# A graph layer on one core: row norm by statistics instructions, and one ScalarE activation per block of nodes

## The chip, the core and the metric

The kernel runs on one core of a Trainium2 chip. The metric is the time of one execution on the device in microseconds. The core has five engines that run their own queues in order and meet through semaphores: PE (TensorE, matmuls), DVE (VectorE), ACT (ScalarE), POOL (GpSimd) and SP (SyncE, here only an issuer of DMAs). ACT and POOL issue DMAs too.

## What is computed

One layer of a graph network with 6,250 nodes, 64 features and 206,250 edges, sorted by their target:

```python
h = jnp.maximum(_layernorm(x, axis=-1), 0.0)          # (6250, 64), no scale, no shift
msg = h[src] + edge_attr_64                            # (206250, 64)
agg = jax.ops.segment_sum(msg, dst, num_segments=6250)
y = jax.nn.relu(agg @ W1 + b1) @ W2 + b2               # 64 -> 128 -> 64
return x + y
```

`_layernorm` is `(x - mean) / sqrt(var + 1e-5)` along the 64 features.

## The kernel before

**The main stage.** The sum over edges of `h[src]` is made without a gather for most edges. Tiles of three target nodes have up to 128 edges each; for each tile a table of counts (how often each source occurs for each target) is built by a matmul of one-hot codes. Six tiles are one step, and there are 311 steps (0 to 310). In step `n`, `count(n)` does six matmuls into PSUM (L839), and ACT copies the counts into `ring` (L845). DVE makes the one-hot rows `hot` ahead of that (`encode` and `rows_of_tiles`, L806 to L825). Fourteen steps make a block of 252 target nodes; from step 16 on, `products` multiplies the counts of the block before by the normed features `h2` (L857). The edges' own features are summed by one-hot matmuls (`chunk_sum`, L423), with the features loaded by `load`. The 24 last groups of edges are handled differently: POOL gathers rows of `h` from a table in memory and adds them to the edges' features (`fetch_h`, 188 indirect DMAs of L283), and PE sums them (`features_h`, L479). When a pair of such groups comes into PE's order is set by a planner: `clock(n)` gives the assumed start of step `n`, `pool[0]` the assumed time on POOL, which starts at `clock(2) + OPENING_US`, each gather counts 2.0 us, and a pair is taken at one of the steps 5 and 11 of a block for which its last gather is 4 us past. The program's order is written out by hand on every engine, and each engine keeps to it.

**The opening.** Before step 0 the kernel

- loads targets (`dstn`, `firsts_i`), sources (`src`) and `x` (`xl`, by SP in one piece of 6,144 rows and a rest);
- finds for every third target node in which row of 256 targets it begins (`firsts` to `row_i`, matmuls `pf` of L270 and L271), fetches these rows in 15 indirect DMAs (`fetch_row`), and searches them on ACT (`seek`, a Sign activation with a sum, L298); `place` (DVE, L303 and L305) turns the result into edge numbers, three rows at a time;
- transposes the sources on PE (`psrc`, L561), copies them on ACT (L562), packs them with the targets into one word each on DVE (L572), and writes the words to memory (`packed`); `fetch_pair` gathers words by the found edge numbers, `unpack_pair` (DVE, L648 to L667) splits them, and `turn` transposes the digits on PE (`pk`, `pw`) and copies them on ACT into `kq` (L688) and `kv` (L692, an Exp);
- finds where the chunks of edges begin (`chunk_starts`, `chunk_rows`, `chunk_columns`, `chunk_index`);
- norms `x`. The nodes are laid out as 128 partitions by HI = 49 blocks of 64 features, taken in three parts of 16, 16 and 17 blocks.

The norm before takes these steps, all on wide tiles: `norm_mean` (DVE, one reduction over the 49 blocks, L502), `norm_center` for each part (DVE, subtracts the mean, L507; ACT squares, L509), `norm_var` (DVE, a reduction for each part, L514), `norm_root` (DVE, then Sqrt on ACT, L518), `norm_scale` (DVE, reciprocal and one Newton step, L522 to L526), and `norm_h` for each part (DVE, L530: maximum with 0, times the reciprocal root; then SP writes the part to `table`, L531, from which POOL gathers).

The program order ahead of step 0 before, after the norm's root:

```python
    fetch_pair(0)
    ...
    for f in unpack_pair(0):
        f()
    chunk_rows(0, 2 * RC)
    load(0)
    chunk_columns(0, 2, "pc", 2)
    turn(0, P, columns(0))
    seek(9, 3)
    norm_scale()
```

`before` in the code is a dictionary of work that is put ahead of the named step: `seek(12, 3)` ahead of step 1, for instance.

Of the kernel before, what the change touches and what calls it, by code (L numbers as in the profile page):

```python
# [22 lines left out]
P = 128  # L23
# [92 lines left out]
OPENING_US = 8.0  # L116
# [3 lines left out]
def gnn_kernel(ctx: ExitStack, tc: tile.TileContext, x, src_t, dst_t, dst_g, edge, w1, b1, w2, b2, out):  # L120
# [52 lines left out]
    nc.sync.dma_start(xl[:, :HI - 1, :], x[:N - N % P, :].rearrange("(h l) d -> l h d", l=P))  # L173
# [62 lines left out]
    for q in range(JQ):  # L236
# [14 lines left out]
    stat_at = rows_at + 11 * L1  # L251
    assert stat_at + 4 * HI <= junk_at
# [14 lines left out]
                            iota_v.unsqueeze(1).to_broadcast([P, NR, P]), op=OP.is_lt)  # L267
    pf = ps.tile([P, IC], F32, tag="po", name="pf", bufs=1)
# [223 lines left out]
    stat = agg[:, stat_at:stat_at + 4 * HI].rearrange("p (k h) -> p k h", k=4)  # L492
    mean, var, rs, t = (stat[:, k, :] for k in range(4))
    thirds = [(0, 16), (16, 32), (32, HI)]

    squares = {}

    def wide(a, h0, h1):
        return a[:, h0:h1].unsqueeze(2).to_broadcast([P, h1 - h0, D])

    def norm_mean():
        nc.vector.tensor_reduce(mean, xh, AX.X, OP.add)  # L502
        nc.vector.tensor_scalar(mean, mean, 1.0 / D, None, op0=OP.mult)

    def norm_center(k):
        h0, h1 = thirds[k]
        nc.vector.tensor_tensor(xh[:, h0:h1], xh[:, h0:h1], wide(mean, h0, h1), op=OP.subtract)  # L507
        part = agg[:, squares_at + h0 * D:squares_at + h1 * D].rearrange("p (h d) -> p h d", d=D)
        nc.scalar.activation(part, xh[:, h0:h1], AF.Square)  # L509
        squares[k] = part  # L510

    def norm_var(k):
        h0, h1 = thirds[k]
        nc.vector.tensor_reduce(var[:, h0:h1], squares.pop(k), AX.X, OP.add)  # L514

    def norm_root():
        nc.vector.tensor_scalar(var, var, 1.0 / D, EPS, op0=OP.mult, op1=OP.add)
        nc.scalar.activation(t, var, AF.Sqrt)  # L518

    def norm_scale():  # L520

        nc.vector.reciprocal(rs, t)  # L522
        nc.vector.tensor_tensor(t, rs, rs, op=OP.mult)
        nc.vector.tensor_tensor(t, t, var, op=OP.mult)
        nc.vector.tensor_scalar(t, t, -0.5, 1.5, op0=OP.mult, op1=OP.add)
        nc.vector.tensor_tensor(rs, rs, t, op=OP.mult)  # L526

    def norm_h(k):
        h0, h1 = thirds[k]
        nc.vector.scalar_tensor_tensor(xh[:, h0:h1], xh[:, h0:h1], 0.0, wide(rs, h0, h1), op0=OP.max, op1=OP.mult)  # L530
# [21 lines left out]
    for i in range(6):  # L552
        fetch_row(i)
    srcf = src.bitcast(F32)
    nc.scalar.activation(srcf, src, AF.Copy)
    srcv = srcf.rearrange("p (q h j) -> p q h j", h=2, j=J)
    for h in range(2):
        n = (GA + 1 - h) // 2
        pt = ps.tile([P, J, P], F32, tag="pc", name="psrc")
        for j in range(J):  # L560
            nc.tensor.transpose(pt[:n, j, :], srcv[:, :n, h, j], ident)  # L561
        nc.scalar.activation(srcl[:n, h].rearrange("q p j -> q j p"), pt[:n], AF.Copy)  # L562
# [5 lines left out]

    nc.vector.tensor_scalar(begins_i, begins_i, P - 1, None, op0=OP.bitwise_and)
# [6 lines left out]
    identb = consts.tile([P, P], BF16, name="identb")  # L576
# [12 lines left out]
    pools[0].__exit__(None, None, None)  # L589
    ring = ctx.enter_context(pools[1]).tile([P, HI, (STEPS + FRESH) * SC], F32R, name="ring")  # L590
    nc.vector.tensor_copy(identb, ident)
# [391 lines left out]
    for g in range(GA, GA + 2):  # L983
        load_h(g)
    for i in range(11, IC):
        fetch_row(i)
# [299 lines left out]
```

## Time and profile before

| | |
|---|---|
| time, median of 3 runs | 512.6 us (511.7 to 514.32) |
| the profiled execution | 512.52 us, span 510.8 us |
| mean granted TensorE clock | 0.95 |
| busy: PE, DVE, ACT, POOL | 422.9, 352.7, 350.8, 367.2 us |
| chain that ended last, by engine | PE 67%, ACT 13%, DVE 13%, issue 6%, DMA 1% |

A row of the timeline gives the start in microseconds from the span's start, the time busy, the engine, the line of the code, the operation, what it writes and reads, and the count of merged instructions; in brackets stands how long the engine was idle before and what ended that. `PEld` is the weight load of PE, and a name with q, such as SPq, is that engine's issuing of DMAs. The row PE of the page gives the busy share in 40 slices of 12.8 us, in tenths. `issue` is a wait that the profile ties to nothing.

### The profile page before, as it was taken

The page shows a single profiled execution, that of the slowest core. Times are in us where ns is not written, and L with a number is a line of the kernel's source. Part 1 is how long each engine was busy: PE and PEld are TensorE (multiplying, and loading weights), DVE is VectorE, ACT ScalarE, POOL GpSimd, SP SyncE. Part 2 cuts the span into 40 slices and gives each one's busy share as a digit, 9 for nine tenths or more (in the row PEclk, how much of TensorE's full clock was granted, in tenths as well). Part 3 has the DMA queues.
Part 4 walks back from the last instruction along what each step waited for, and adds up shares of the span by engine and source line. Part 5 has one row for each costly group of instructions (what it writes and reads, how often), then busy time and mean ns, then how long its engine had stood idle before and what let it go on. Part 6 is the DMA issues. An engine that isn't in the chain of part 4 may idle for free.

```text
span 510.8 us, 17235 instructions
## 1 busy us (share of the span) xinstructions
PE 422.9 (83%) x7194; PEld 375.3 (73%) x7195; DVE 352.7 (69%) x776; ACT 350.8 (69%) x517; POOL 367.2 (72%) x260
## 2 busy tenths in 40 slices
PE   3024689898889998989999998998999999998985
PEld 3023587887878888878788886887887788887964
DVE  4799858877596865776649756788566875577621
ACT  4528977677666767768587777778777756776650
POOL 6756838888885888888888888888888888870000
PEclk9656989999989998999999999999999989999998
DMA  8848537577474673856748757568659557474310
GB/s 226 239 132 285 135 81 184 140 188 169 115 180 103 159 198 85 228 126 149 208 76 204 178 112 216 134 138 242 143 119 247 118 114 182 109 189 138 119 37 15
DMA packets 113355, 78.65 MB, mean 154 GB/s; under 512 B 32736, under 2 KB 108632, under 8 KB 113048
## 3 DMA queue, kind: packets, MB, share of 16 engines
q1 hardware_dynamic: 84356, 65.87, 43.3%
q0 software_dynamic: 28624, 10.11, 16.6%
q10 hardware_dynamic: 292, 1.52, 0.9%
q8 instruction: 58, 0.95, 0.8%
q14 instruction: 25, 0.20, 0.1%
HBM read 73.48 MB, written 3.99 MB: 152 GB/s over the span
## 4 chain that ended last, share of the span: by engine, by line
PE 67%; ACT 13%; DVE 13%; issue 6%; DMA 1%; DVEq 0%; ACTq 0%
PE pv L857 24%; PE pc L839 21%; PE bank L423 10%; ACT ring L845 6%; DVE hot L825 3%; PE bank L479 2%; ACT kq L688 2%; PE po L935 2%; PE ph L927 2%; PE pv L452 2%; ACT kv L692 1%; DVE sums L888 1%; DVE hotf L410 1%; DMA firsts_i<-in_dst_g 1%; PE pk L681 1%
## 5 line engine op out<-in xcount | busy, mean ns | idle before, releaser
L283 POOL DMA_INDIRECT pfeat<-table,src_p x188 | 319.7, 1701 | 60.5 <-issue 50.0
L845 ACT ACTIVATE ring<-pc 128x882 fp32r<-128x882 f32 x310 | 276.2, 923 | 90.9 <-PE pc L839 73.7
L839 PE MATMUL pc<-hot 128*128 128x147 fp8e4 x1862 | 174.0, 232 | 30.3 <-ACT ring L845 16.5
L825 DVE TENSOR_TENSOR hot<-at,of 128x576 int32<-128x576 bf16 x208 | 163.1, 825 | 40.0 <-PE pc L839 26.8
L857 PE MATMUL pv<-ring,h 128*128 128x252 f32 (+1 forms) x1078 | 172.5, 297 | 1.1 <-ACT ring L849 0.9
L839 PEld LDWEIGHTS <-hot 128*128 128x128 fp8e4 x1862 | 127.5, 100 | 51.9 <-issue 29.8
L857 PEld LDWEIGHTS pv<-ring,h 128*128 128x128 f32 x1078 | 141.3, 193 | 1.6 <-ACT ring L849 1.1
L423 PE MATMUL bank<-feat,hotf 128*18 128x64 f32 x3168 | 66.4, 223 | 11.6 <-DVE hotf L410 5.4
L423 PEld LDWEIGHTS bank<-feat,hotf 128*18 128x18 f32 x3168 | 50.5, 99 | 25.3 <-issue 8.7
L888 DVE TENSOR_TENSOR sums<-sums,pv 128x252 f32<-128x252 f32 (+4 forms) x34 | 10.0, 322 | 60.6 <-PE pv L857 59.2
L410 DVE TENSOR_TENSOR hotf<-rel,iota 128x432 f32<-128x432 bf16 (+1 forms) x67 | 39.8, 593 | 0.0
L688 ACT ACTIVATE kq<-pk 128x512 bf16<-128x512 f32 (+18 forms) x48 | 18.3, 448 | 17.4 <-PE pk L681 13.8
L806 DVE TENSOR_TENSOR at<-iota_a,kq 128x576 bf16<-128x576 bf16 (+1 forms) x52 | 23.5, 452 | 2.7 <-ACT kq L688 2.4
L283 POOL DMA_INDIRECT words<-packed,first_i x15 | 19.1, 1276 | 4.6 <-issue 3.4
L812 DVE TENSOR_TENSOR of<-of,kv 128x432 bf16<-128x432 bf16 (+1 forms) x52 | 20.0, 384 | 3.0 <-ACT kv L692 0.2
L927 PE MATMUL ph<-sums,w1s 128*128 128x252 f32 (+3 forms) x52 | 16.9, 413 | 6.0 <-DVE sums L888 2.0
L940 DVE TENSOR_TENSOR after<-po,after 126x128 f32<-126x128 f32 (+3 forms) x26 | 7.5, 287 | 19.4 <-PE po L935 18.5
L283 POOL DMA_INDIRECT sums<-in_dst_g,row_i x15 | 15.4, 1024 | 7.0 <-issue 4.3
L929 ACT ACTIVATE after<-ph,b1s 128x252 f32<-128x252 f32 (+3 forms) x26 | 11.9, 467 | 11.4 <-PE ph L927 11.2
L806 DVE TENSOR_TENSOR of<-iota_w,kq 128x432 bf16<-128x432 bf16 (+1 forms) x52 | 19.4, 373 | 0.0
L935 PE MATMUL po<-w2s,after 128*126 128x64 f32 (+3 forms) x104 | 15.5, 273 | 0.2 <-ACT rel L376 0.2
L324 PE MATMUL pstart<-begins,first 128*1 128x9 f32 (+2 forms) x30 | 1.5, 172 | 17.0 <-DVE sums L502 9.3
(183 smaller groups left out, 313.5 us busy)
## 6 DMA issues: line engine op xcount, KB each, us to landing
feat<-in_edge SPq DMA_DIRECT2D x132, 384.0 KB
pfeat<-in_edge SPq DMA_DIRECT2D x23, 256.0 KB
pfeat<-table,src_p POOLq DMA_INDIRECT x188
out_y<-after SPq DMA_DIRECT2D x23, 63.0 KB
dstn<-in_dst_g SPq DMA_DIRECT2D x1, 1024.0 KB
table<-xl SPq DMA_DIRECT2D x2, 512.0 KB
after<-in_x SPq DMA_DIRECT2D x4, 252.0 KB
packed<-dstn ACTq DMA_DIRECT2D x1, 768.0 KB
```

The source lines that it names most:

```text
L283: nc.gpsimd.indirect_dma_start(out=rows, out_offset=None, in_=source, in_offset=bass.IndirectOffsetOnAxis(ap=index, axis=0), compute_op=op)
L410: nc.vector.tensor_tensor(hot_of[u][:, :n].rearrange("p c j w -> p (c j) w"), rel[:, c:c + n].rearrange("p c q k -> p (c q k)").unsqueeze( ...
L423: nc.tensor.matmul(bank[q * QP:q * QP + WQ, at:at + D], hot[:, c, j, :], feat[c][:, j, :], start=(k == 0), stop=(k == JP - 1))
L688: nc.scalar.activation(kq[:, q, at:at + n].rearrange("s i k o -> s (i k) o"), pk[:, q, a:a + n].rearrange("s i k -> s (i k)").unsqueeze(2) ...
L806: nc.vector.tensor_tensor(to[:, :n].rearrange("s i k (m o) -> s (i k) m o", o=2), iota_k.rearrange("s (m o) -> s m o", o=2).unsqueeze(1).t ...
L812: nc.vector.tensor_tensor(pairs_of, pairs_of, kv[:, c:c + n].rearrange("s i k o -> s (i k) o").unsqueeze(2) .to_broadcast([P, 2 * n, WE // ...
L825: nc.vector.tensor_tensor(hot[:, :n, c:c + m * A8].rearrange("s i (w a) -> s i w a", a=A8), at[:, o:o + n, k].unsqueeze(2).to_broadcast([P ...
L839: nc.tensor.matmul(pc[:, k, q * K:(q + 1) * K], hot[:, i, :P], hot[:, i, P:P + K], start=True, stop=True)
L845: nc.scalar.activation(to.rearrange("p h (k m) -> p h k m", k=2), pc[:, :, :ST // 2 * K].rearrange("p k (m h) -> p h k m", h=HI), AF.Copy)
L857: nc.tensor.matmul(pvs[b], h2[:, h, :], ring[:, h, c:c + columns_of_block(b)], start=(h == 0), stop=(h == HI - 1))
L927: nc.tensor.matmul(ph[:, :n], w1s, agg[:, start[b]:start[b + 1]], start=True, stop=True)
L935: nc.tensor.matmul(po[:pairs[b], k, :], hid[:, k:2 * pairs[b]:2], w2s, start=True, stop=True)
```

## The change

Four things are changed.

1. The norm's mean and variance come from `bn_stats`, a DVE instruction that gives count, mean and sum of squared deviations of the even and of the odd elements of a block: one instruction for each of the 49 blocks (`norm_sums`). `norm_root` joins the halves by five more small operations, and `norm_scale` makes `shifted = -mean * rs` by one more. `norm_mean`, `norm_center` with its Square on ACT, and `norm_var` go.
2. `norm_h` becomes one ACT activation for each block, `Relu(rs * x + shifted)`, in place of one wide DVE operation for each part: 49 activations of 128x64 instead of three operations on DVE. An Exp of one column is put behind the root.
3. `x` is loaded in three parts and the rest.
4. The order is written anew. The first half of the sources is transposed ahead of the `pf` matmuls. Nine rows are fetched ahead of the first words instead of six and five. The three `norm_sums` stand between the searches. `chunk_rows`, `norm_scale`, `norm_h(0)` and the chunk columns come ahead of unpacking and turning the first words; `norm_h(1)` comes behind the turn, and `norm_h(2)` ahead of step 1; the searches of the last six rows come ahead of step 3, the loads of the gathered groups' features behind `load(1)`. `OPENING_US` of the planner is 11 instead of 8.

```diff
-OPENING_US = 8.0
+OPENING_US = 11.0
...
-    nc.sync.dma_start(xl[:, :HI - 1, :], x[:N - N % P, :].rearrange("(h l) d -> l h d", l=P))
+    for h0, h1 in ((0, 16), (16, 32), (32, HI - 1)):
+        nc.sync.dma_start(xl[:, h0:h1, :], x[h0 * P:h1 * P, :].rearrange("(h l) d -> l h d", l=P))
...
+    def turn_sources(h):
+        n = (GA + 1 - h) // 2
+        pt = ps.tile([P, J, P], F32, tag="pc", name="psrc")
+        for j in range(J):
+            nc.tensor.transpose(pt[:n, j, :], srcv[:, :n, h, j], ident)
+        nc.scalar.activation(srcl[:n, h].rearrange("q p j -> q j p"), pt[:n], AF.Copy)
+
+    turn_sources(0)
     pf = ps.tile([P, IC], F32, tag="po", name="pf", bufs=1)
...
-    def norm_mean():
-        nc.vector.tensor_reduce(mean, xh, AX.X, OP.add)
...
-    def norm_center(k):
...
-    def norm_var(k):
...
+    def norm_sums(k):
+        for h in range(*thirds[k]):
+            nc.vector.bn_stats(halves[:, h, :], xh[:, h, :])
 
     def norm_root():
+        nc.vector.tensor_tensor(apart, halves[:, :, 1], halves[:, :, 4], op=OP.subtract)
+        nc.vector.tensor_tensor(total, halves[:, :, 1], halves[:, :, 4], op=OP.add)
+        nc.vector.tensor_tensor(var, halves[:, :, 2], halves[:, :, 5], op=OP.add)
+        nc.vector.tensor_tensor(apart, apart, apart, op=OP.mult)
+        nc.vector.scalar_tensor_tensor(var, apart, D / 4.0, var, op0=OP.mult, op1=OP.add)
         nc.vector.tensor_scalar(var, var, 1.0 / D, EPS, op0=OP.mult, op1=OP.add)
         nc.scalar.activation(t, var, AF.Sqrt)
...
         nc.vector.tensor_tensor(rs, rs, t, op=OP.mult)
+        nc.vector.scalar_tensor_tensor(shifted, total, -0.5, rs, op0=OP.mult, op1=OP.mult)
 
     def norm_h(k):
         h0, h1 = thirds[k]
-        nc.vector.scalar_tensor_tensor(xh[:, h0:h1], xh[:, h0:h1], 0.0, wide(rs, h0, h1), op0=OP.max, op1=OP.mult)
+        for h in range(h0, h1):
+            nc.scalar.activation(xh[:, h, :], xh[:, h, :], AF.Relu, bias=shifted[:, h:h + 1], scale=rs[:, h:h + 1])
         nc.sync.dma_start(table.rearrange("(l h) d -> l h d", l=P)[:, h0:h1, :], xh[:, h0:h1])
...
-    for i in range(6):
+    for i in range(9):
         fetch_row(i)
...
-    seek(0, 6)
-    norm_mean()
+    seek(0, 3)
+    norm_sums(0)
     place(0, 3)
-    for i in range(6, 11):
-        fetch_row(i)
-    for k in range(3):
-        norm_center(k)
-        seek(6 + k, 1)
+    seek(3, 3)
+    norm_sums(1)
     place(3, 3)
-    for k in range(3):
-        norm_var(k)
+    norm_sums(2)
+    seek(6, 3)
     norm_root()
+    nc.scalar.activation(root, zero, AF.Exp)
...
     fetch_pair(0)
-    for g in range(GA, GA + 2):
-        load_h(g)
-    for i in range(11, IC):
+    for i in range(9, IC):
         fetch_row(i)
     place(6, 3)
     chunk_starts(0, 2 * RC, "pc", 2)
-    src_hi = late.tile([P, GP * J], I32, tag="part", name="src_hi")
-    table_rows(src_p, src_hi)
-    for f in unpack_pair(0):
-        f()
     chunk_rows(0, 2 * RC)
     load(0)
+    norm_scale()
+    norm_h(0)
     chunk_columns(0, 2, "pc", 2)
-    turn(0, P, columns(0))
-    seek(9, 3)
-    norm_scale()
     chunk_index(0, 2)
     fetch_dst(0)
     fetch_pair(2)
-    for k in range(3):
-        norm_h(k)
+    for f in unpack_pair(0):
+        f()
+    turn(0, P, columns(0))
     load(1)
-    for g in range(GA + 2, GA + 4):
+    norm_h(1)
+    src_hi = late.tile([P, GP * J], I32, tag="part", name="src_hi")
+    table_rows(src_p, src_hi)
+    for g in range(GA, GA + 4):
         load_h(g)
     rows_of_tiles(0)
 
     before = {
-        1: [lambda: seek(12, 3), lambda: chunk_nodes(0)],
-        2: [lambda: [fetch_h(g) for g in range(GA, GA + 4)], lambda: chunk_turn(0)],
-        3: [lambda: place(9, 3)],
+        1: [lambda: norm_h(2)],
+        2: [lambda: [fetch_h(g) for g in range(GA, GA + 4)], lambda: chunk_nodes(0)],
+        3: [lambda: chunk_turn(0), lambda: seek(9, IC - 9)],
+        4: [lambda: place(9, 3)],
         5: [lambda: place(12, 3)],
```

More of the change, by code (lines that the diff above doesn't have):

```diff
@@ L550, in clear @@
         nc.scalar.activation(agg[:, a:z], zero.to_broadcast([P, z - a]), AF.Copy)
-    for i in range(6):
+    for i in range(9):
         fetch_row(i)
[L554 to L562, printed above, removed]
+    turn_sources(1)
+    identb = consts.tile([P, P], BF16, name="identb")
     firstp = small.tile([1, GP], F32, name="firstp")
```

26 lines of the change are left out of this document (9 added, 17 removed).

## The prediction

> **What bounds the kernel now.** I read the page's slices first, then the busy times by stretch, then the chain of waits in order of time, and last the timeline of the opening, engine by engine. The change touches only the first part of the kernel and a planner constant, so the question is what sets the time there, and whether a delay there reaches the end.
>
> ```profile
> span 510.8 us, 17235 instructions
> ...
> PE   3024689898889998989999998998999999998985
> ...
> 30.00:37.00 7.00, 2.04 (x10) 2.06 (x11) 6.32 (x28) 0.00 (x0) 2.13 (x4) 0.50 0.23 64
> ...
> 45.00:60.00 15.00, 9.87 (x164) 7.82 (x163) 14.65 (x28) 14.86 (x27) 12.51 (x7) 0.84 0.59 150
> ...
> 60.00:80.00 20.00, 16.75 (x297) 15.50 (x297) 11.87 (x35) 15.29 (x17) 10.80 (x7) 0.91 0.40 99
> ...
> 47.82 2.40 ACT ring L845 x3
> ...
> 65.63 1.02 ACT ring L845
> ...
> 67.55 1.37 PE pv L857 x6
> ```
>
> The rows that begin with a stretch (30.00:37.00) give its length, then PE, PEld, DVE, ACT and POOL busy. From 67.55 us the slices show PE at 0.8 to 1.0 for the rest, so the end is the moment at which step 16 (the first products) can begin, plus a PE-bound remainder of fixed work. Before it there are two stages. Up to about 37 us DVE carries the path (6.32 of 7 us busy while ACT does nothing). From the first count to 67 us ACT carries it: 14.86 of 15 us busy, and the chain runs from ring copy to ring copy, while PE has a third of its time free. An instruction more on ACT's queue in this second stage is a delay of all that follows.
>
> ```profile
> 37.58 1.09 ACT L688 ACTIVATE kq<-pk 128x512 bf16<-128x512 f32 x2 [7.86 <-PE pk L681]
> 38.68 1.28 ACT L692 ACT_TABLE_LOAD   x1
> 39.98 0.69 ACT L692 ACTIVATE kv<-pw,ln_one 128x512 bf16<-128x512 f32 x1
> ...
> 43.98 0.92 ACT L845 ACTIVATE ring<-pc 128x882 fp32r<-128x882 f32 x1 [1.57 <-issue]
> ...
> 47.71 4.41 ACT L845 ACTIVATE ring<-pc 128x882 fp32r<-128x882 f32 x5
> ```
>
> In this window ACT has only two things to give back: the table load, and 1.57 us of waiting ahead of the first ring copy. Later it has nothing idle until past 67 us.
>
> **What leaves DVE and what comes.**
>
> ```profile
> 18.03 3.42 DVE L502 TENSOR_REDUCE sums<-xl 128x49 f32<-128x3136 f32 x1 [2.36 <-DMA xl<-in_x]
> ...
> 21.91 3.59 DVE L507 TENSOR_TENSOR xl<-xl,sums 128x1024 f32<-128x1024 f32 x3
> ...
> 25.69 3.53 DVE L514 TENSOR_REDUCE sums<-sums 128x16 f32<-128x1024 f32 x3
> ...
> 36.61 3.55 DVE L530 SCALAR_TENSOR_TENSOR xl<-xl,sums 128x1024 f32<-128x1024 f32 x3
> ...
> 8.97 0.17 DVE L278 TENSOR_SCALAR middle<-row 128x15 f32<-128x15 f32 x1
> 9.05 0.17 DVE L280 TENSOR_SCALAR nhalf<-nfirst 128x15 f32<-128x15 f32 x1
> ...
> 35.22 0.21 DVE L523 TENSOR_TENSOR sums<-sums 128x49 f32<-128x49 f32 x1
> ...
> 35.46 0.21 DVE L524 TENSOR_TENSOR sums<-sums 128x49 f32<-128x49 f32 x1
> ```
>
> The four wide passes sum to 3.42 + 3.59 + 3.53 + 3.55 = 14.1 us. In their place stand 49 statistics instructions of 64 elements, which no trace shows. Lower bound: independent small ones start 0.08 us apart (8.97 to 9.05, 15 elements), and 49 further elements at the 1.09 ns of the wide reduction (3.42 us for 3136) make 0.13 us. Upper bound: an operation that waits for the one before it takes 0.24 us (35.22 to 35.46), and if each must also empty six results, some 0.30. I take 0.17, nearer to the lower end since the 49 don't depend on each other: 8.3 us. Six more small operations on 49 elements cost at most 6 x 0.22 = 1.3 us. DVE is freed of some 14.1 - 9.6 = 4.5 us.
>
> How much of it advances the first turn? The new order puts the lists' search in the way: place(3,3) stands on DVE between the second and third statistics, and it waits for ACT's search of six rows.
>
> ```profile
> 22.46 0.51 ACT L298 ACTIVATE sums<-sums,nhalf 128x256 bf16<-128x256 int32 x1 [0.22 <-DMA sums<-in_dst_g,row_i]
> ...
> 29.50 0.15 DVE L303 SCALAR_TENSOR_TENSOR first<-first,middle 128x3 f32<-128x3 f32 x1
> ...
> 29.69 0.38 DVE L305 TENSOR_SCALAR first_i<-first 128x3 int32<-128x3 f32 x1
> ...
> 30.77 0.29 DVE L648 TENSOR_SCALAR code<-words 128x256 int16<-128x256 int16 x1
> ...
> 33.85 0.29 DVE L667 TENSOR_SCALAR code<-code 128x512 int16<-128x512 int16 x1
> ...
> 34.05 0.21 DVE L330 TENSOR_SCALAR starts<-pstart 1x64 f32<-1x64 f32 x1
> ...
> 34.41 0.41 DVE L339 TENSOR_TENSOR quarters<-starts,row_e 1x256 f32<-1x256 f32 x1
> ...
> 34.74 0.44 DVE L522 RECIPROCAL sums<-sums 128x49 f32<-128x49 f32 x1
> ...
> 36.29 0.61 PE L681 MATMUL pk<-identb,code 128*128 128x128 bf16 x2
> ...
> 36.54 0.15 DVE L354 COPY cols<-pcols 128x1 f32<-128x1 f32 x1
> ```
>
> The sixth row is searched at 22.46 because it landed only then (its bracket names the DMA). The search ends at 23.0, and I let it slip to 23.3, since the first transposes now stand on PE ahead of the matmuls that give the rows' numbers. From there DVE's path is: place 0.4; 17 statistics x 0.17 = 2.9; root with six small operations 1.1; place and PE's row starts 0.7; chunk_rows 0.4 (34.05 to quarters); scale with its extra product 1.6 (34.74 to 36.14, and 0.2); quarters, PE's columns and chunk_index 2.3 (34.41 to 36.69); unpacking 3.4 (30.77 to 34.14). That is 23.3 + 12.8 = 36.1 us. From PE's first pk to the first kq passed 1.3 us (36.29 to 37.58), so kq starts at 37.4 against 37.58: the saving on DVE is spent, because scale and columns now stand ahead of the unpacking and not beside PE's turn. With 0.13 us a block it is 0.7 us earlier, with 0.30 us 2.2 us later, and a further 1 us since the second statistics then overrun the search. norm_h(0) on ACT lies in the seven idle microseconds ahead of kq and costs nothing: 16 x 0.31 = 5.0 us against the 7.0 us (2.3 + 3.4 + 1.3) between the end of scale and kq. Were that cover gone, it would cost its 5.0 us.
>
> **What comes to ACT.** These rows price ACT's short operations:
>
> ```profile
> L692 ACT ACTIVATE kv<-pw,ln_one 128x16 bf16<-128x16 f32 x1 | 0.3, 323 | 0.0
> ...
> L688 ACT ACTIVATE kq<-pk 128x16 bf16<-128x16 f32 x2 | 0.3, 216 | 0.0
> ...
> 56.16 0.28 ACT L688 ACTIVATE kq<-pk 128x16 bf16<-128x16 f32 x2
> ...
> 56.29 0.32 ACT L692 ACTIVATE kv<-pw,ln_one 128x16 bf16<-128x16 f32 x1
> ...
> 56.45 0.97 ACT L845 ACTIVATE ring<-pc 128x882 fp32r<-128x882 f32 x1
> ...
> 17.00 0.51 ACT L298 ACTIVATE sums<-sums,nhalf 128x256 bf16<-128x256 int32 x1 [2.57 <-DMA sums<-in_dst_g,row_i]
> 17.42 0.19 ACT L298 ACTIVATION_READ_ACCUMULATOR sums<-sums,nhalf 128x1 f32 x1
> ```
>
> The Square passes leave (ACT did them beside DVE's center and reductions, off the path), and so does the table load at 38.68: kv would overlap kq's end by some 0.15 us as the short pair does (56.16 + 0.28 against 56.29), and the load, now at the root, is hidden in ACT's idle time. That is worth 39.98 - 38.67 + 0.15 = 1.4 us, rounded down. What comes are 49 activations of 128x64, each with a scale and a bias read from a column; 16 of them stand between kv and the first ring copy, 17 between the first and the second.
>
> A short activation with a bias column holds the queue 0.16 us (56.29 to 56.45, 16 elements); 48 elements more at about 0.84 ns make 0.20, the lower bound, if the second column is free. A column lengthens the short form by 323 - 216 = 107 ns, so a second one gives 0.31. The search shows a dearer bias column: 0.42 us for 256 elements (17.00 to 17.42), less 192 x 0.84 ns, plus the second column, 0.36, the upper bound. I take 0.31, the sum from the row that is nearest in size. 33 x 0.31 = 10.2 us.
>
> The Trainium skill speaks against this step. Its page "ScalarE: Activation LUTs" (What ACT_TABLE_LOAD costs) gives 186 ns and 0.833 ns an element, 93 ns more for each column operand, and 93 ns of overlap between neighbours; by it, as an estimate, a block costs 0.33 us, 33 cost 11.0 us, and the result would be 0.8 us later than mine. By the same section a change of tables costs 2.66 us with its drain; the trace shows the load at 1.28 us and kv 0.02 us behind it, so the measured 1.4 us stands.
>
> **The sum.** ACT's queue from kq to the second stage's end: + 10.2 for the blocks, - 1.4 for the table, - 1.57 for the wait that the blocks fill, - 0.2 for the earlier kq: + 7.0 us. The six searches stand in this window before and after, and cancel. PE has no work that could catch this up: behind 67.55 us it is busy throughout.
>
> The rest comes at nothing. The two extra loads of x are two more issues on SP; the weights behind them have no early reader. Without them DVE waited 2.36 us for x at 18.03, but now the search is the later wait. load_h moved behind load(1) must land ahead of the first gather. That gather waits for the last part of the table, which now leaves behind norm_h(2), so POOL's 188 gathers start some 7 us late, as does PE:
>
> ```profile
> 45.64 1.60 POOL L283 DMA_INDIRECT pfeat<-table,src_p  x1 [3.42 <-DMA table<-xl]
> ...
> 93.83 1.13 PE L479 MATMUL bank<-after,pfeat 128*64 128x42 f32 x32
> ```
>
> By the planner's sums OPENING_US of 11 moves the first group's matmuls from step 33 to step 39 and the last pair's from 299 to 305, inside the 311 steps; the tail's blocks stay. If POOL were later than PE by more than that, PE would wait at L479, 1 us for each. The profiled execution took 512.52 us (span 510.8 and 1.7 around it), the median 512.6. Forecast: 512.5 + 7.0 = 519.5 us.
>
> **The rivals.** First, cheap blocks: the second column is free (0.20 us) and a statistic costs 0.13. 6.6 - 3.0 - 0.2 - 0.7 = + 2.7, about 515.2 us. For it: the short kq show only 0.07 us between starts. Against: every column in the trace has a price. Second, dear statistics at 0.30: 3.2 us on top, 522.7 us. For it: nothing shows this instruction. Against: even 49-element operations that wait for one another start 0.24 us apart. Third, the other side: DVE and not ACT bounds the opening, and the 4.5 us that it is freed of come through: 508.0 us. Place: steps 0 to 15. For it: DVE is 14.65 of 15 us busy there, hardly less than ACT. Against: the chain names ring copies. It decides where ACT's blocks cost less than what ACT gets back, 33 x 0.09 us = 3.0 us; the short kq's 0.07 us with 48 elements more makes 0.11, close to it.
>
> **The numbers.** One measurement can tell about 0.5%, 2.6 us, from no change. The forecast has 0.51, dear statistics 0.16, cheap blocks 0.21 (half of it under 515.2, and so no change), DVE as the bound 0.12. So faster 0.12, same 0.11, slower 0.77. The range from 511.5 to 524 leaves out the third rival and the far end of the second; the forecast's own is 516 to 522.
>
> **What would show it.** Right: Relu activations start about 0.31 us apart; the first kq starts near 37.4 us; the first ring copy stands near 44 us as before, but the fifth some 7 us later; PE's first product at 74 to 75 us; ACT without idle time in between. Wrong: the blocks 0.2 us apart or less, the first kq before 34 us, or the first product no later than 68 us. If the first product moves but the end doesn't, the PE-bound remainder had slack that I don't see.

## The result, and the profile after

The changed kernel took 528.96 us (median of 4 executions, 527.81 to 529.12), the kernel before 512.69 us (4 executions, 511.7 to 514.32) in the same measurement: ratio 1.0309, 95% interval 1.0279 to 1.0340. Slower, as forecast, but by 16.3 us where 7.0 were forecast, and outside the range. The ratios here and below leave out executions more than 1.5% above the fastest of their kernel; the medians leave out none, and the trace of late_rows on the slow chip is of such an execution.

The experiments ran on four chips, and the chips differ: the kernel before took 498.1 and 497.0 us on two of them, which are called quick below, and 514 to 516 us on two others, called slow. Which chip the first measurement ran on is not on record; by its 512.7 us it is nearer to the slow ones.

The DVE row of the page before:

```profile
DVE  4799858877596865776649756788566875577621
```

and the slices of the page after, to be read against those of before:

```profile
span 527.4 us, 17319 instructions
...
PE   3003368999789898997989998998999989998985
...
DVE  5537295886777866678567776696576766577711
ACT  5429997777766668767767887787687666877730
```

PE's rise comes later (its first 8 stands in the seventh slice, not in the sixth), and DVE's third slice, 26 to 40 us, is busy for 0.3 of the time where it was 0.9 before: DVE, which was to carry the path there, is idle most of the time. Its timeline shows with what; the columns are start, duration, and in brackets the idle time ahead and its releaser:

```profile
20.78 2.12 DVE L512 BATCH_NORM_STATS2 sums<-xl 128x6 f32<-128x64 f32 x16
...
23.14 1.23 DVE L512 BATCH_NORM_STATS2 sums<-xl 128x6 f32<-128x64 f32 x9
25.18 0.35 DVE L512 BATCH_NORM_STATS2 sums<-xl 128x6 f32<-128x64 f32 x2 [0.81 <-issue]
26.61 0.23 DVE L512 BATCH_NORM_STATS2 sums<-xl 128x6 f32<-128x64 f32 x1 [1.07 <-issue]
27.31 0.23 DVE L512 BATCH_NORM_STATS2 sums<-xl 128x6 f32<-128x64 f32 x1 [0.48 <-issue]
28.01 0.23 DVE L512 BATCH_NORM_STATS2 sums<-xl 128x6 f32<-128x64 f32 x1 [0.47 <-issue]
...
35.09 0.24 DVE L516 TENSOR_TENSOR sums<-sums 128x49 f32<-128x49 f32 x1 [4.06 <-remote]
```

Sixteen statistics take 2.12 us. The first nine of the last 17 run at that pace too. The other eight come singly or in pairs, 0.70 us apart or a multiple of it, with "issue" as the releaser, that is, waiting for nothing the profile shows; "remote" is a semaphore event that the profile ties to no instruction. From 24.4 to 35.1 us DVE does less than 2 us of work. This is called the pause below.

ACT's timeline of the same kernel:

```profile
38.65 5.41 ACT L536 ACTIVATE xl<-xl,sums 128x64 f32<-128x64 f32 x16 [0.61 <-DVE sums L531]
44.71 1.08 ACT L684 ACTIVATE kq<-pk 128x512 bf16<-128x512 f32 x2 [0.66 <-issue]
45.68 0.69 ACT L688 ACTIVATE kv<-pw,ln_one 128x512 bf16<-128x512 f32 x1
46.25 5.40 ACT L536 ACTIVATE xl<-xl,sums 128x64 f32<-128x64 f32 x16
51.55 0.90 ACT L841 ACTIVATE ring<-pc 128x882 fp32r<-128x882 f32 x1
52.34 5.73 ACT L536 ACTIVATE xl<-xl,sums 128x64 f32<-128x64 f32 x17
57.96 1.69 ACT L841 ACTIVATE ring<-pc 128x882 fp32r<-128x882 f32 x2
...
63.59 1.69 ACT L841 ACTIVATE ring<-pc 128x882 fp32r<-128x882 f32 x2
```

The 33 blocks behind kv hold ACT for (57.96 - 46.25) - 0.79 (the ring copy, 52.34 - 51.55) = 10.9 us, and from the first kq to the ring copy of step 3 ACT has no gap. The first kq stands 7.1 us later than before (44.71 against 37.58), the ring copy of step 3 15.1 us later (63.59 against 48.5). The two delays stay nearly whole: the last ring copy is 13.9 us later. The end adds 2.7 us, since the last products run at a granted clock of 0.50. The rows are the timeline of PE after, and a window of it with PE, PEld, DVE, ACT and POOL busy, then the clock:

```profile
512.06 6.41 PE L853 MATMUL pv<-ring,h 128*128 128x294 f32 x33
...
509.00:515.80 6.80, 6.80 (x29) 6.06 (x30) 0.00 (x0) 0.00 (x0) 0.00 (x0) 0.50 0.00 0
```

Before, the same 33 products took 4.76 us, at a granted clock of 1.00 (495 to 501 us). This is not a mark of the change: of the three traces of the unaltered changed kernel two have it (6.41 and 6.24 us) and one has not (4.75 us), and of the three traces of the kernel before one has it (6.34 us).

### The profile page after: what moved, and what is told of

The parts are those of the page before. It is cut to its first block, busy times and chain, and to the rows that moved or that the text cites. A ratio compares the mean times of both kernels' runs of the same rounds, so it can differ in the third digit from the quotient of the medians.

```text
span 527.4 us, 17319 instructions
## 1 busy us (share of the span) xinstructions
PE 427.0 (81%) x7194; PEld 377.9 (72%) x7195; DVE 346.7 (66%) x820; ACT 364.6 (69%) x564; POOL 366.8 (70%) x260
## 4 chain that ended last, share of the span: by engine, by line
PE 62%; ACT 16%; DVE 11%; issue 7%; POOL 1%; DMA 1%; another core or an unknown queue 1%; DVEq 0%; ACTq 0%; POOLq 0%
PE pv L853 23%; PE pc L835 19%; PE bank L436 9%; ACT ring L841 6%; DVE hot L821 3%; ACT xl L536 3%; PE bank L492 2%; ACT kq L684 2%; PE po L931 2%; PE ph L923 2%; PE pv L465 2%; ACT kv L688 2%; DVE sums L884 1%; DVE hotf L423 1%; DMA sums<-in_dst_g,row_i 1%
## 5 line engine op out<-in xcount | busy, mean ns | idle before, releaser
L436 PE MATMUL bank<-feat,hotf 128*18 128x64 f32 x3168 | 68.1, 224 | 12.1 <-DVE hotf L423 5.4
L684 ACT ACTIVATE kq<-pk 128x512 bf16<-128x512 f32 (+18 forms) x48 | 18.3, 445 | 10.9 <-PE pk L677 8.1
L802 DVE TENSOR_TENSOR at<-iota_a,kq 128x576 bf16<-128x576 bf16 (+1 forms) x52 | 23.5, 451 | 3.4 <-ACT after L443 1.9
L296 POOL DMA_INDIRECT words<-packed,first_i x15 | 16.9, 1125 | 4.6 <-issue 4.3
L337 PEld LDWEIGHTS pstart<-begins,first 128*1 128x1 f32 x30 | 0.9, 81 | 24.9 <-DVE first L316 13.1
```

Of the source, the lines that this page charges most:

```text
L296: nc.gpsimd.indirect_dma_start(out=rows, out_offset=None, in_=source, in_offset=bass.IndirectOffsetOnAxis(ap=index, axis=0), compute_op=op)
L436: nc.tensor.matmul(bank[q * QP:q * QP + WQ, at:at + D], hot[:, c, j, :], feat[c][:, j, :], start=(k == 0), stop=(k == JP - 1))
L684: nc.scalar.activation(kq[:, q, at:at + n].rearrange("s i k o -> s (i k) o"), pk[:, q, a:a + n].rearrange("s i k -> s (i k)").unsqueeze(2) ...
L802: nc.vector.tensor_tensor(to[:, :n].rearrange("s i k (m o) -> s (i k) m o", o=2), iota_k.rearrange("s (m o) -> s m o", o=2).unsqueeze(1).t ...
```

## The experiments

The question was first what makes the pause, then whether the forecast holds without it. The edits are against the changed kernel unless it is said otherwise.

**Four versions on a quick chip** (before 498.1 us, 19 executions). Four theories of the pause were open: the statistics instruction itself, a limit on rows of short instructions ("burst"), the landing of transfers, and the gathers that GpSimd issues there. The times that were expected suppose a chip like that of the first measurement.

early_sums: the statistics of parts 0 and 1 in a row, those of part 2 ahead of the second place.

```
     seek(0, 3)
     norm_sums(0)
+    norm_sums(1)
     place(0, 3)
     seek(3, 3)
-    norm_sums(1)
-    place(3, 3)
     norm_sums(2)
+    place(3, 3)
```

> Only the order on DVE changes: the first two thirds of the statistics (32 instructions) run together ahead of place(0,3), the last 17 between place(0,3) and place(3,3). Burst theory (DVE takes some 27 short instructions at 0.13 us each and then only one per 0.7 us, whatever they are): the 32 slow down after about 27, near 17.5 us, end at 20 to 22 us instead of 18.3, and the last 17 are slow again; first kq near 40 us, time 523 to 526. Gather theory (POOL's row gathers from 24 us on hold DVE up): all 49 are done at about 23 us without a pause, first kq near 35 us, time 518 to 521. Landing theory (the last third of x comes late): the last 17 wait as before and end near 35 us, time unchanged at 529.

late_rows: the rows 9 to 14 gathered later.

```
     fetch_pair(0)
-    for i in range(9, IC):
-        fetch_row(i)
     ...
     fetch_pair(2)
+    for i in range(9, IC):
+        fetch_row(i)
```

> The gathers of rows 9 to 14 stand behind the second pair of words on POOL, at 43 to 51 us instead of 25 to 33 us; DVE's order is that of the changed kernel. Gather theory: the last statistics run at 0.13 us and end near 25.5 us, first kq near 35.5 us, time about 520. Burst theory and landing theory: the last statistics still end near 35 us, first kq near 44.7 us, time 528 to 530.

plain_third: the last 17 statistics as reductions, so that the kernel leaves out the statistics of these nodes.

```
+    nc.vector.memset(halves[:, 32:, :], 1.0)
...
-            nc.vector.bn_stats(halves[:, h, :], xh[:, h, :])
+            if k == 2:
+                nc.vector.tensor_reduce(halves[:, h, 2:3], xh[:, h, :], AX.X, OP.max)
+            else:
+                nc.vector.bn_stats(halves[:, h, :], xh[:, h, :])
```

> The last 17 statistics are replaced by 17 reductions (a maximum) over the same 64 elements, so these nodes are normed wrongly; the count of instructions and their place stay. Burst and gather theories: the reductions pause as the statistics did, first kq near 44.7 us, time 528 to 530. If it is the statistics instruction itself: the 17 run at about 0.13 us, first kq near 35.5 us, time about 520.

wide_h: parts 2 and 3 of the nodes normed by two wide operations each on DVE, not by 33 blocks on ACT.

```
+        nc.vector.tensor_scalar(total, total, 0.5, None, op0=OP.mult)
...
     def norm_h(k):
...
+        if k:
+            nc.vector.tensor_tensor(xh[:, h0:h1], xh[:, h0:h1], wide(total, h0, h1), op=OP.subtract)
+            nc.vector.scalar_tensor_tensor(xh[:, h0:h1], xh[:, h0:h1], 0.0, wide(rs, h0, h1), op0=OP.max, op1=OP.mult)
-        for h in range(h0, h1):
+        for h in range(h0, h1) if k == 0 else ():
...
     load(1)
-    norm_h(1)
...
     rows_of_tiles(0)
+    norm_h(1)
```

> The second and third parts of h are made by two wide DVE operations each (subtract the mean, maximum and scale) behind the first one-hot rows, in place of 33 activations of ACT. If ACT's queue carries steps 0 to 2: the first ring copy stands 5.4 us earlier against kq and the fourth 11 us earlier, less what DVE's 5 us hold up; time 518 to 521. If DVE carries these steps: the 5 us on DVE come through and the time falls by 3 us at most, 526. The first kq stays near 44.7 us in both.

None of the four paused, wide_h with the unaltered order of the statistics included. So they can't tell the four theories apart: whatever makes the pause wasn't there. The times were 502.84 us for early_sums (ratio 1.0098, 1.0065 to 1.0132), 501.18 and 503.25 us (one execution each) for late_rows and plain_third, and 501.86 us for wide_h (1.0074, 1.0038 to 1.0111). wide_h was meant to bring the opening back to that of before and didn't. In its timelines of PE and ACT the step's numbers wait for the target words, whose DVE operations now stand behind the wide ones:

```profile
46.46 0.91 PE L388 MATMUL pdst<-shift,dstq 128*128 128x128 f32 x3 [4.61 <-DVE dstq L381]
...
47.41 0.49 ACT L389 ACTIVATE rel<-pdst 128x384 bf16<-128x384 f32 x1 [4.60 <-PE pdst L388]
...
51.46 1.69 ACT L848 ACTIVATE ring<-pc 128x882 fp32r<-128x882 f32 x2
```

**The kernels unaltered, one activation for a part, and a mixture, on a second quick chip** (before 497.0 us, 19 executions).

> The changed kernel once more, unaltered, to be compared with the kernel before on one chip. If the pause of 10 us in the last statistics belongs to the kernel, it is there again, the first kq near 44.7 us, and the ratio to the kernel before is 1.03. If it belongs to the chip or to the circumstances of the first measurement (the kernel with wide operations has the same order up to there and showed no pause), the last statistics end near 25 us, the first kq is near 35 us, the fourth ring copy near 53.5 us, and the ratio is 1.006 to 1.012.

> The kernel before, unaltered, for a trace on the same chip. Theory: its opening is as in the first trace, first kq at 37.6 us and fourth ring copy at 48.5 us, whatever the later steps take; so the changed kernel without the pause is 2 to 3 us earlier at the first kq and 4.5 to 5.5 us later at the fourth ring copy. Rival: the opening itself moves with the chip by several us.

The changed kernel as it is took 503.38 us (4 executions): ratio 1.0139, 1.0077 to 1.0201. Its timelines of DVE and ACT:

```profile
22.83 2.24 DVE L512 BATCH_NORM_STATS2 sums<-xl 128x6 f32<-128x64 f32 x17
25.10 0.24 DVE L516 TENSOR_TENSOR sums<-sums 128x49 f32<-128x49 f32 x1
...
35.33 1.08 ACT L684 ACTIVATE kq<-pk 128x512 bf16<-128x512 f32 x2 [1.05 <-PE pk L677]
...
42.16 0.90 ACT L841 ACTIVATE ring<-pc 128x882 fp32r<-128x882 f32 x1
...
54.20 1.69 ACT L841 ACTIVATE ring<-pc 128x882 fp32r<-128x882 f32 x2
```

No pause: 17 statistics in 2.24 us, kq at 35.33 and not 44.71. Before, on the same chip, took 496.59 us in the traced execution, with kq at 37.51 and the ring copy of step 3 at 48.4, so that its opening is the same on both kinds of chip. Here the changed kernel is 5.8 us later at step 3, 6.6 us at step 100 and 6.9 us at the end of the span (501.7 against 494.8). The medians differ by 6.4 us. That is near the forecast's + 7.0 us, but the agreement is partly luck: two terms of the sum were off in opposite directions, as the next section shows, and the two traces part and meet again on the way. At the last ring copy they are 10.0 us apart (483.5 against 473.5 us), and the end brings 3.1 us back, because in this trace it is the kernel before whose last products ran at the low clock. The scatter between executions is of the same size as such differences, so single microseconds behind step 20 are not told apart.

one_act: parts 2 and 3 by one Relu each, so 2 activations in place of 33; the kernel leaves out scale and shift for these nodes.

```
     def norm_h(k):
+        if k:
+            nc.scalar.activation(xh[:, h0:h1], xh[:, h0:h1], AF.Relu)
-        for h in range(h0, h1):
+        for h in range(h0, h1) if k == 0 else ():
```

> norm_h of the second and third part is one Relu activation over the whole part without scale and shift, so these nodes aren't normed; 33 activations of 0.34 us become two of about 1.05 us, all else stays. If ACT's queue carries steps 0 to 3, the fourth ring copy stands 8.5 to 9 us earlier than in the changed kernel (44.5 to 45.5 us without a pause) and the whole is 8 to 9 us faster than the changed kernel, 3 to 5 us faster than the kernel before. If DVE or PE bounds these steps, 4 us at most come through.

497.1 us (10 executions), ratio 1.000 (0.996 to 1.004); kq at 35.38 as in the unaltered kernel, the ring copy of step 3 at 47.57, 6.6 us earlier. ACT's timeline:

```profile
36.92 1.07 ACT L536 ACTIVATE xl<-xl 128x1024 f32<-128x1024 f32 x1
40.13 0.91 ACT L843 ACTIVATE ring<-pc 128x882 fp32r<-128x882 f32 x1 [2.15 <-issue]
40.94 1.10 ACT L536 ACTIVATE xl<-xl 128x1088 f32<-128x1088 f32 x1
...
47.57 1.69 ACT L843 ACTIVATE ring<-pc 128x882 fp32r<-128x882 f32 x2
```

The two Relu hold ACT 1.07 and 1.10 us in place of the 10.9. Of these 8.7 us less, 2.15 turn into idle time ahead of the first ring copy, and the other 6.6 us bring step 3 forward. That is less than the 8.5 to 9 us expected there, and the kernel is as fast as the one before, not 3 to 5 us faster; but it is the whole slowdown on that chip.

mixed: early_sums and wide_h together, the two groups of searches drawn ahead so that ACT isn't idle, and the target words' operations ahead of the second wide part.

```
     turn(0, P, columns(0))
+    seek(9, 3)
     ...
-        1: [lambda: norm_h(2)],
-        2: [lambda: [fetch_h(g) for g in range(GA, GA + 4)], lambda: chunk_nodes(0)],
-        3: [lambda: chunk_turn(0), lambda: seek(9, IC - 9)],
+        1: [lambda: seek(12, 3), lambda: chunk_nodes(0)],
+        2: [lambda: norm_h(2), lambda: [fetch_h(g) for g in range(GA, GA + 4)]],
+        3: [lambda: chunk_turn(0)],
```

> Statistics, h of the first part on ACT as in the changed kernel, with the early order of the statistics; h of the other parts by two wide DVE operations each; the searches of rows 9 to 14 back at the kernel before's places, and chunk_nodes ahead of the last part. If both readings hold (the pause is no part of the order, ACT's queue is what the blocks cost), the first kq is at 34 us, the fourth ring copy at 44 to 47 us, and the whole 1 to 4 us faster than the kernel before. If DVE bounds steps 0 to 6, its 5 us of wide operations come through and the time is the kernel before's or 1 to 2 us above.

495.94 us (10 executions), ratio 0.9959 (0.9931 to 0.9988): a little faster than the kernel before on that chip.

**The same on a slow chip** (before 514.5 us, 7 executions). In the expectations from here on "first square root" stands for the first kq (44.71 us in the first measurement), and in the second of them "third ring copy" for that of step 3.

> The changed kernel unaltered, on a third occasion. Open: what stretched the last 17 statistics of norm_sums from 2.2 to 12 us in the first measurement and not in the runs since. If it belongs to the circumstances in which everything runs slower (the kernel before at about 512 us, its matmuls of L423 at 66 us of busy time in place of 59), it returns only where those are seen: the ratio to before is then 1.03 and the first square root starts near 44 us. If the kernel before is near 497 us here, the statistics take about 2.2 us, the first square root starts near 35.3 us and the ratio is 1.012 to 1.015. If the pause is a matter of chance from execution to execution, the times of this kernel scatter by about 9 us from round to round.

> The kernel before unaltered, for its opening beside the run above on the same occasion. First square root near 37.5 us and third ring copy near 48.4 us in either case, since the reductions take longer each than an issue pause; 497 us in the quick circumstances, 512 in the slow ones.

> Sums of parts 0 and 1 together ahead of place(0, 3), those of part 2 ahead of place(3, 3). If the pause hits dense statistics wherever they stand, 32 statistics in a row are hit harder here and the time is no better than that of the changed kernel. If it hits one place in the instruction stream or one moment of the span, the first square root comes at about 34 us without a pause. Without any pause on this occasion: ratio to before about 1.010, as in the earlier comparison.

> Early sums, parts 2 and 3 normed by two wide DVE operations each, and two searches drawn ahead, as in the earlier run that gave 0.996. The theory that ScalarE's 33 blocks set the opening expects 0.993 to 0.999 again in either circumstances; if the earlier result was a matter of that one occasion, it is above 1.000 here.

The pause is back. The unaltered changed kernel took 534.41 us, ratio 1.0415 (1.0288 to 1.0542); its DVE timeline has this:

```profile
23.02 1.61 DVE L512 BATCH_NORM_STATS2 sums<-xl 128x6 f32<-128x64 f32 x12
24.98 0.23 DVE L512 BATCH_NORM_STATS2 sums<-xl 128x6 f32<-128x64 f32 x1 [0.35 <-issue]
25.69 0.23 DVE L512 BATCH_NORM_STATS2 sums<-xl 128x6 f32<-128x64 f32 x1 [0.48 <-issue]
...
32.13 0.24 DVE L516 TENSOR_TENSOR sums<-sums 128x49 f32<-128x49 f32 x1 [4.09 <-remote]
```

Before, beside it, took 516.39 us with kq at 37.66: no pause there. The early sums don't help any more, 530.50 us, ratio 1.0339 (1.0236 to 1.0442), and their DVE timeline says why:

```profile
14.01 4.14 DVE L512 BATCH_NORM_STATS2 sums<-xl 128x6 f32<-128x64 f32 x32
...
21.14 2.24 DVE L512 BATCH_NORM_STATS2 sums<-xl 128x6 f32<-128x64 f32 x17
...
28.98 0.26 DVE L520 SCALAR_TENSOR_TENSOR sums<-sums 128x49 f32<-128x49 f32 x1 [2.63 <-remote]
30.38 0.19 DVE L521 TENSOR_SCALAR sums<-sums 128x49 f32<-128x49 f32 x1 [1.14 <-issue]
...
33.90 0.17 DVE L318 TENSOR_SCALAR first_i<-first 128x3 int32<-128x3 f32 x1 [3.25 <-remote]
```

The statistics are all done by 23.4 us, and what pauses are the small operations that follow. So it isn't the statistics instruction, and with 32 of them in a row at full pace it isn't a limit on the length of a row. The mixture pauses in the same place and gave 520.83 us, 1.0204 (1.0092 to 1.0316), not the 0.993 to 0.999 that was expected.

**A place in the stream, or a moment?** In the paused runs so far the pause lay within DVE's recorded instructions 75 to 93 and, but for its start at 23.5 us in the early sums and the mixture, within 24 to 35.3 us; either could be what it hangs on. Both runs are on a second slow chip (before 515.1 us), one execution each.

```
     nc.vector.memset(srcl[64:96], FAR << DST_BITS)
+    pad = small.tile([P, 1], F32, name="pad")
+    for _ in range(24):
+        nc.vector.memset(pad, 0.0)
```

> 24 memsets of one column more on DVE at about 4 us, where DVE waits 1.66 us for firsts_i; nothing reads them. About 1.5 us of DVE time, hidden there. Theory of the place in the stream: the pause keeps its place by count, so it moves 24 instructions back: it falls on the second group of statistics (which starts at 20.7 us and ran in 2.11 us until now) and the third group runs clean; the first square root comes at 40 to 41 us in place of 44.5. Theory of the moment: the second group runs clean in 2.1 us and the third pauses from 24.4 us on as before, first square root near 44.5 us. If the kernel before takes about 497 us on this occasion, neither shows and the first square root is near 35.3 us.

```
+    pad = small.tile([P, 1], F32, name="pad")
+    nc.vector.tensor_reduce(pad, xl[:, :, :].rearrange("p h d -> p (h d)"), AX.X, OP.max)
     norm_sums(2)
```

> One reduction more on DVE ahead of the last 17 statistics (3.4 us, over all of x, into a column that nothing reads). Theory of the place in the stream: the pause moves 3.4 us later with its instructions, from 27.8 to 38.5 us, first square root near 48 us. Theory of the moment: the reduction covers the first 2 us of it, the pause still ends near 35 us, first square root near 44.5 to 45 us. Without a pause on this occasion: first square root near 38.7 us.

The DVE timeline with 24 instructions put ahead:

```profile
21.22 2.12 DVE L515 BATCH_NORM_STATS2 sums<-xl 128x6 f32<-128x64 f32 x16
...
23.77 1.10 DVE L515 BATCH_NORM_STATS2 sums<-xl 128x6 f32<-128x64 f32 x8
25.28 0.23 DVE L515 BATCH_NORM_STATS2 sums<-xl 128x6 f32<-128x64 f32 x1 [0.41 <-issue]
...
35.95 0.25 DVE L519 TENSOR_TENSOR sums<-sums 128x49 f32<-128x49 f32 x1 [2.65 <-remote]
```

The second group runs clean and the third pauses from 24.9 us on, as before: the theory of the place falls. And with 3.4 us put ahead of the third group:

```profile
22.73 3.42 DVE L583 TENSOR_REDUCE pad<-xl 128x1 f32<-128x3136 f32 x1
26.06 1.35 DVE L512 BATCH_NORM_STATS2 sums<-xl 128x6 f32<-128x64 f32 x10
28.46 0.23 DVE L512 BATCH_NORM_STATS2 sums<-xl 128x6 f32<-128x64 f32 x1 [1.04 <-issue]
...
35.55 0.24 DVE L516 TENSOR_TENSOR sums<-sums 128x49 f32<-128x49 f32 x1 [1.24 <-DVE sums L512]
```

The pause still ends at 35.5 us, and the first kq comes at 45.18 us: the added 3.4 us cost 0.5 to 1.3 against the 44.71 and 43.86 of the unaltered kernel, which was not run on this chip. The times were 532.23 and 533.99 us.

**What happens at that moment: the gathers** (a slow chip, before 515.9 us, 12 executions). GpSimd issues its gathers 1.25 us apart until 32.5 us and then waits. late_rows was run again, and a kernel that gathers the rows 9 to 14 twice:

```
-    for i in range(9, IC):
-        fetch_row(i)
+    for _ in range(2):
+        for i in range(9, IC):
+            fetch_row(i)
```

> Rows 9 to 14 gathered behind the second pair of words, on an occasion where the unaltered kernel pauses (before near 514 us; if before is near 497 us nothing can be told). Theory of the gathers: no pause in the 17 statistics, first square root near 35 us in place of 44.5, ratio to before 1.012 to 1.02 in place of 1.03 to 1.04. Theory of the moment without the gathers (something else at 24 to 35 us): pause and first square root as they were, 44 us or later.

> Rows 9 to 14 gathered twice, the second time over the first with the same words: six gathers of 1.25 us more on GpSimd, issued from about 32.8 to 40.3 us. Theory of the gathers: the pause lasts up to 7.5 us longer and takes in the root, the index steps and the unpacking; first square root near 50 us. Theory without the gathers: DVE runs clean from 35 us on, the first square root stays near 44.5 us.

The timelines of POOL and DVE with the rows late:

```profile
24.09 0.94 POOL L296 DMA_INDIRECT words<-packed,first_i  x1 [0.30 <-issue]
...
25.92 0.23 DVE L512 BATCH_NORM_STATS2 sums<-xl 128x6 f32<-128x64 f32 x1 [0.50 <-issue]
26.61 0.99 DVE L512 BATCH_NORM_STATS2 sums<-xl 128x6 f32<-128x64 f32 x7 [0.46 <-issue]
```

and with the rows twice:

```profile
39.04 0.95 POOL L296 DMA_INDIRECT sums<-in_dst_g,row_i  x1 [0.30 <-issue]
...
39.32 0.24 DVE L516 TENSOR_TENSOR sums<-sums 128x49 f32<-128x49 f32 x1 [6.86 <-remote]
...
42.82 0.21 DVE L520 SCALAR_TENSOR_TENSOR sums<-sums 128x49 f32<-128x49 f32 x1 [1.89 <-remote]
```

The end of the pause follows the last gather of the row. The unaltered kernel and the mixture with early rows are those of the earlier measurement on the same chip; mixed_late, the mixture with late rows, follows below:

| | last gather ends | DVE runs clean from | first kq | ring copy, step 3 |
|---|---|---|---|---|
| rows late | 25.0 | 26.6 | 37.26 | 56.1 |
| unaltered | 32.5 | 35.0 | 43.86 | 62.7 |
| rows twice | 40.0 | 42.8 | 51.93 | 70.8 |
| mixture, rows late | 25.1 | 26.8 | 35.93 | 49.5 |
| mixture, rows early | 32.2 | 34.5 | 42.66 | 52.3 |

Six gathers of 1.25 us are 7.5 us; moving them behind brings step 3 forward by 6.6 us, doubling them puts it back by 8.1. late_rows took 524.08 us, ratio 1.0142 (1.0070 to 1.0213), in place of 1.0415, which is near the ratio of the changed kernel on the quick chip (1.0139). A pause of some 2 us stays, beside the two gathers of words, so that kq came at 37.26 and not at the expected 35. The rows gathered twice took 535.78 us; of the 8.1 us the last ring copy kept 3.5, and the end none that a single run could show.

mixed_late: the mixture with the rows gathered as in late_rows and their searches ahead of steps 2 and 3.

```
+        1: [lambda: chunk_nodes(0)],
+        2: [lambda: norm_h(2), lambda: seek(9, 3), lambda: [fetch_h(g) for g in range(GA, GA + 4)]],
+        3: [lambda: chunk_turn(0), lambda: seek(12, 3)],
```

> Early sums and the two wide operations for parts 2 and 3 as in the earlier version, with the rows 9 to 14 gathered behind the second pair of words and their searches ahead of steps 2 and 3. Theory of the gathers: no pause before 35 us, first square root near 34 us, ratio 0.995 to 1.003 where the same version with the early gathers gave 1.020. Theory without the gathers: 1.02 again.

517.13 us (10 executions), ratio 1.0056 (1.0011 to 1.0100), where the mixture with the early rows gave 1.0204. The interval reaches above the expected 1.003; kq came at 35.93 us, 6.7 us earlier than in the mixture with early rows on this chip, and 1.9 us later than the 34.03 of the mixture on the quick chip, so some 2 us of pause are left. No version beat the kernel before on both kinds of chip.

## Why the prediction was half right

**What held: the place, the sign, and the term for ACT.** The 33 blocks hold ACT 10.9 us, 0.33 us each, against 0.31 taken. The estimate from the figures of the Trainium skill ("ScalarE: Activation LUTs", What ACT_TABLE_LOAD costs), 0.33 us, agrees. From the first kq to the ring copy of step 3 the kernel before takes 48.5 - 37.58 = 10.9 us, the changed one 63.59 - 44.71 = 18.9 us, and on the quick chip 54.20 - 35.33 = 18.9 us: + 8.0 us where the sum had + 10.2 - 1.4 - 1.57 = + 7.2. The forecast's mark "the first ring copy near 44 us, the fifth some 7 us later" was 42.2 us and 5.8 us on the quick chip, and "PE's first product at 74 to 75 us" was 72.7 us there; in the first measurement it was 51.6, 15.1 and 82.1 us. The size on the quick chip is partly luck: at step 3 the sum had + 7.2 - 0.2 = + 7.0 us, and the trace has + 8.0 - 2.2 = + 5.8 us, a dearer block against a cheaper path on DVE.

**What failed: the term for DVE, "17 statistics x 0.17 = 2.9", and with it "kq 0.2 us earlier".** In the measured execution these 17 and the wait behind them took from 23.14 to 35.09 us, 12.0 us, and kq came 7.1 us later. The price of the instruction was not the reason: without the pause 17 take 2.24 us, 0.13 each, the lower bound, and kq comes 2.2 us earlier than before (35.33 against 37.51, both on the quick chip). The step that failed is the assumption behind the whole DVE sum, that an instruction's price and its waits on others are all there is. Every row from which the sum was made was one of the kernel before, where DVE works on wide tiles (3.4 to 3.6 us a line of the page) until 29.2 us while GpSimd gathers. I listed no rival in which other engines' work slows the issue of short instructions, though the change puts short ones in the place of long ones beside the same gathers. Of the two unforeseen parts, the pause is (44.71 - 35.33) = 9.4 us of kq, and the half clock in the last products 2.7 us of the end. That the first hangs on the gathers is shown by experiment; the second is only seen, and it comes and goes between traces of either kernel.

**The rivals.** Dear statistics (522.7 us) has the right direction and the wrong cause; cheap blocks had the price of the statistics right (0.13 us) and is refuted by 0.33 us a block. DVE as the bound is refuted by one_act: with 31 activations fewer and DVE's work as it was, step 3 came 6.6 us earlier. The point that "PE has no work that could catch this up" is not settled by single traces: from step 3 to the last ring copy 15.1 us became 13.9 and 5.8 us became 10.0, but the 8.1 us of the rows gathered twice became 3.5.

**The gathers** into the features started 16 us late (61.73 against 45.64), not some 7, and cost nothing that could be seen: the group of PE's products that read their rows (L492) shows 0.9 us of idle time ahead of it in the whole span, 0.7 before.

## What to carry to other kernels

Replacing a few wide instructions by many short ones must be priced beside what the other engines issue in that stretch, not from the engine's own rows alone: on some chips a dense row of short DVE instructions lost its pace while GpSimd issued gathers, and the kernel with wide ones showed no such loss there. Moving a bundle of work to an idle engine pays only as far as that engine's queue is free at that point: the 33 activations in ACT's busy stretch cost most of their time (8.7 us less of them gave 6.6 us), the 16 in ACT's waiting time nothing (on the quick chip kq still waited 1.05 us for PE behind them). And a difference of 1% to 3% is worth a second chip before it is explained, since the same two kernels stood at 1.014 in one measurement and at 1.031 and 1.042 in two others.

## What the runs showed of the hardware

In the first measurement and on the two slow chips, DVE instructions of 0.13 us that wait for nothing started 0.70 us apart, or a multiple of it, while GpSimd issued indirect gathers 1.25 us apart; on the two quick chips the same program ran them 0.13 us apart beside the same gathers at the same pace. Whether this belongs to the chip or to the occasion is not told apart.

The gathers are not enough by themselves. Gathers run from 9.8 us on, yet on a slow chip early_sums ran 32 statistics in 4.14 us from 14.0 us and 17 in 2.24 us from 21.1 us, and in the kernel before some 13 short operations from 29.3 us on ran beside its last gathers without a pause. No such loss of pace began before 23.2 us. What starts it no run shows.

One rival is untested: the recording of the trace. Every execution on record has a span and a clock from the profiler, so none shows the kernel unrecorded, and the traces that pause hold fewer records of semaphore updates: for the unaltered changed kernel 5,942 in the first measurement and 5,840 on the slow chip against 9,017 on the quick one, and between 24 and 35 us 25 and 30 against 261. The kernel before has as few of them on the slow chip (5,838) and no pause, so this is a companion of the slow chips and not shown as a cause. If it is the cause, part of the slowdown there is one of the measurement.

The Trainium skill ("SBUF — State Buffer", SBUF: two separate sides) has a lock between DVE and GpSimd, held for a whole instruction, by which some DVE operations keep GpSimd from writing its descriptors. POOL's timeline of the kernel before has one row that would fit that direction, a gather that takes 2.02 us beside the wide DVE operations; seven others beside them (18.0 to 28.8 us) keep 0.95 us, so it shows no rule:

```profile
24.29 2.02 POOL L283 DMA_INDIRECT words<-packed,first_i  x1 [0.30 <-issue]
...
31.62 0.95 POOL L283 DMA_INDIRECT sums<-in_dst_g,row_i  x1 [0.30 <-issue]
```

The pause runs the other way: the gathers keep their 0.95 us and DVE waits. Blocking for the whole of a gather would space DVE's starts by 1.25 us and not by 0.70. Which resource it is, and why only some measurements show it, stays open; the granted clock is not the reason, since the run with 24 instructions put ahead paused at a granted clock of 1.0 in the opening and the unaltered kernel of the first measurement at 0.5, and early_sums on the quick chip ran without a pause at 0.5.
